# Counting a group's destination nodes from any 32-node quarter, and summing its messages by 32 columns of the array

## The chip, the cores and the metric

The kernel runs on one core of a Trainium2 chip. The metric is the device time of one execution in microseconds (us); the median of three executions of the kernel before is 4363.7 us (4302.89 to 4385.22). The profile is of another single execution, whose span is 3774.9 us; that is some 589 us shorter than the median, and no view of the profile says where the timed executions spend the difference.

## What is computed

Four graph layers in a row work on 6250 nodes with 64 features and 206,250 edges, sorted by destination node. Three of them are sums over neighbours with fixed weights. The third of the four, in which the change lies, makes a message for each edge from the edge's own 64 attributes and from the features of its source node, and takes the root of the mean of the squared messages at each destination:

```python
x = jax.nn.relu(E @ mlp_w1 + mlp_b1)
x = jax.nn.relu(x @ mlp_w2 + mlp_b2)
scale = jax.nn.sigmoid(x @ Bw + Bb)
shift = x @ Cw + Cb
msg = scale * Vp[src] + shift
M = jnp.power(jnp.clip(msg, EPS, None), ALPHA)
ssum = jax.ops.segment_sum(M, dst, num_segments=n)
```

## The kernel before

The nodes are padded to 49 blocks of 128 (`NB = 49`, `P = 128`), in 7 chunks of 7 blocks. Layers one, two and four multiply by a dense adjacency matrix `A`, which the kernel builds in the first 680 us and keeps in memory; their matmuls are those of `spread` (L732), with 64 columns of the TensorE array for each and two column halves in turn. The third layer is a stage of its own, from L1039 on, and the profile has it from 1125 to 3280 us.

That stage goes through 202 groups of 1024 edges (`G`, `J = 8` edges for each of 128 partitions). For each group g:

- GpSimd (POOL) issues 8 indirect DMAs (L1195), one for each j, which fetch the rows of `Vp_dram` of 128 source nodes into the tile `v`. `v` has four buffers.
- TensorE transposes the edge attributes (L1203), runs the two small layers (L1207, L1211) and the products that give scale and shift (L1216, L1220); ScalarE evicts in between.
- VectorE forms the message from `gate`, `v` and the shift (L1225 to L1227); ScalarE squares it, and VectorE and ScalarE split the square into three bfloat16 parts `m3` (L1229 to L1233), 192 values for an edge.
- VectorE makes `to` (L1238): for each edge a row of zeros with a one at its destination, as a comparison of a counter `count` with `rel_b`, the destination less the group's origin.
- TensorE sums the messages by destination (L1246): `to` is the stationary operand, 128 edges by 128 nodes, `m3` the moving one, and the sums of a block of 128 nodes collect in one PSUM bank, `acc[b]`. When the last group that may lead to a block is through, VectorE reduces the three parts into `H` (L1250), and after seven blocks `finished` does the rest for a chunk.

The edges are sorted, so a group of 1024 edges leads to about 31 nodes in a row. `window(g)` gives a range that holds them, with 32 nodes to spare at either end, and it counts in whole blocks of 128: of the 202 groups, 150 have a window of two blocks and 52 of one. So `to` has 2048 or 1024 elements in each partition, and L1246 runs 16 or 8 matmuls; 2816 in all.

Between the groups, `some_of` deals out other work: comparisons of blocks of A with their transposes (`crossed`, L1136 and L1139) and partial sums for the fourth layer (`partial`, L732 and L1152). The text of the loop isn't the order of the instructions: the framework's scheduler moves them on each engine, so that TensorE's work for group g+1 stands among that for group g. [...]

Ahead of the stage, GpSimd fills `origin` and `width` (L1082) with one memset for each run of groups of the same value, and VectorE subtracts the origin from all destinations (L1085 to L1093) and counts those that fall outside their window in `missed`; if there were any, another program (`general`) would do the whole work again.

Of the kernel before, what the change touches and what calls it, by code (L numbers as in the profile page):

```python
# [9 lines left out]
BF16 = mybir.dt.bfloat16  # L10
# [3 lines left out]
OP = mybir.AluOpType  # L14
AX = mybir.AxisListType

P = 128
N = 6250
D = 64
NB = 49  # L20
NP = NB * P
CB = 7
NC = NB // CB
W = CB * P
E = 206250
J = 8
# [564 lines left out]
CW = 448  # L591
CS = NP // CW
SG = 8
DRIFT = 32


def window(g):

    per = N / E
    lo = max(int(g * P * J * per) - DRIFT, 0) // P  # L600
    hi = min(int((g + 1) * P * J * per) + DRIFT, NP - 1) // P
    return lo, hi - lo + 1


# [1 line left out]
def fast(ctx, tc, bad, x, src, dst, edge_attr, W3, b3, W4, b4, w1, b1, w2, b2, Bw, Bb, Cw, Cb,  # L606
         pAw, pAb, pBw, pBb, out):

    nc = tc.nc
# [129 lines left out]
    with ExitStack() as ph:  # L739

        ipool = ph.enter_context(tc.tile_pool(name="ipool", bufs=1))
        with ExitStack() as first:
# [11 lines left out]
            hi = dpool.tile([P, K1], I32, name="hi")  # L754
# [14 lines left out]
        count = ipool.tile([P, 128, GQ], BF16, name="count")  # L769
# [40 lines left out]
        with ExitStack() as ps:  # L810
# [18 lines left out]
            for c in range(GC):  # L829
# [13 lines left out]
                for k in range(2):  # L843
# [8 lines left out]
                                    op=OP.add)  # L852
# [65 lines left out]
            for s in range(CS):  # L918
                strip = spool.tile([P, NB, CW], BF16, name="strip")
                for q in range(NQ):  # L920
                    at = (s * CW // 2) + q * GB
                    lo = opool.tile([P, GB // GQ, 128, GQ], BF16, name="lo")
                    hd = opool.tile([P, GB // GQ, 2 * NB, GQ], BF16, name="hd")
                    for t, of, k in ((hd, turns, 0), (lo, count, 1)):
# [114 lines left out]
    with ExitStack() as ph:  # L1039
        cpool = ph.enter_context(tc.tile_pool(name="cpool", bufs=1))  # L1040
# [34 lines left out]

        origin = tpool.tile([P, G], F32, name="origin")
        width = tpool.tile([P, G], F32, name="width")
        for t, value in ((origin, lambda g: window(g)[0] * P), (width, lambda g: window(g)[1] * P)):
            g0 = 0
            for g in range(1, G + 1):  # L1080
                if g == G or value(g) != value(g0):
                    nc.gpsimd.memset(t[:, g0:g], float(value(g0)))  # L1082
                    g0 = g
        rel = tpool.tile([P, G, J], F32, name="rel")
        nc.vector.tensor_tensor(rel, dst_g, origin.unsqueeze(2).to_broadcast([P, G, J]),  # L1085
                                op=OP.subtract)
        rel_b = cpool.tile([P, G, J], BF16, name="rel_b")
# [4 lines left out]
        nc.vector.tensor_add(off, off, rel)  # L1092
        nc.vector.tensor_reduce(missed[:, 1:2], off.rearrange("p g j -> p (g j)"), axis=AX.X,  # L1093
                                op=OP.add)
        count = cpool.tile([P, 2 * P, J], BF16, name="count")
        nc.gpsimd.iota(count, pattern=[[1, 2 * P], [0, J]], base=0, channel_multiplier=0,
                       allow_small_or_imprecise_dtypes=True)

        before.close()
        mpool = ph.enter_context(tc.tile_pool(name="mpool", bufs=3))  # L1100
# [53 lines left out]
        todo, crossings = [], []  # L1154
# [13 lines left out]
        def some_of(left):  # L1168

            n = -(-len(todo) // max(left, 1))  # L1170
            for _ in range(n):
                f, *args = todo.pop(0)
                f(*args)
# [13 lines left out]

        plan(FIRST, False)
        last = {b: g for g in range(G) for b in range(window(g)[0], sum(window(g)))}
        ends = [last[c * CB + CB - 1] for c in range(NC)]  # L1190
        acc = {}
        for g in range(G):
            v = mpool.tile([P, J, D], F32, name="v", bufs=4)
            for j in range(J):
# [20 lines left out]
            for b in range(2):  # L1215
                nc.tensor.matmul(p_bc[:, 4 * b:4 * b + 4].rearrange("p j o f -> p (j o f)"), ones,  # L1216
                                 BC_b, start=True, stop=False)
                for k in range(2):
                    q = 2 * b + k
# [13 lines left out]
            nc.vector.tensor_sub(m3[:, :, 2, :], m, m3[:, :, 1, :])  # L1233

            some_of(min(k for k in ends if k >= g) + 1 - g)
            b0, nb = window(g)
            to = mpool.tile([P, 2 * P, J], BF16, name="to")
            nc.vector.tensor_tensor(  # L1238
                to[:, :nb * P, :], count[:, :nb * P, :],
                rel_b[:, g, :].unsqueeze(1).to_broadcast([P, nb * P, J]), op=OP.is_equal)  # L1240
            for b in range(b0, b0 + nb):
                begins = b not in acc
                if begins:
                    acc[b] = ps_s.tile([P, 512], F32, name="p_s")
                for j in range(J):
                    nc.tensor.matmul(acc[b][:, :3 * D], to[:, (b - b0) * P:(b - b0 + 1) * P, j],  # L1246
                                     m3[:, j].rearrange("p t f -> p (t f)"),
                                     start=(begins and j == 0), stop=(last[b] == g and j == J - 1))
                if last[b] == g:
                    nc.vector.tensor_reduce(  # L1250
                        H[:, b, :], acc[b][:, :3 * D].rearrange("p (t f) -> p f t", f=D),
                        axis=AX.X, op=OP.add)
                    if b % CB == CB - 1:
                        finished(b // CB)

        assert not todo and len(crossings) == 28 * CB


        nc.vector.tensor_reduce(missed[:, 2:3], unlike, axis=AX.X, op=OP.add)
# [12 lines left out]
    with ExitStack() as ph:  # L1272
# [5 lines left out]
        for layer in range(3):  # L1278
# [78 lines left out]
```

## Time and profile before

| | |
|---|---|
| median time, three executions | 4363.7 us |
| span of the profiled execution | 3774.9 us |
| busy: PE, DVE, ACT, POOL | 3173.7, 1845.4, 1329.9, 1723.4 us |
| third layer's stage (first to last fetch of `v`) | 1125 to 3280 us, 202 groups |
| granted TensorE clock, whole span | 0.933 |
| L1238 `to` | 202 instructions, 218.8 us |
| L1246 sums by destination | 2816 matmuls |

PE is TensorE's matmuls, PEld its weight loads, DVE VectorE, ACT ScalarE, POOL GpSimd, SP SyncE. A row of a group names the line, the engine, the operation, the tile written and the tiles read, the shape (partitions x elements), and the count; after the bar stand the busy time in us, the mean duration of one in ns, and the idle time of the engine just ahead of these instructions with what ended it. Where matmuls overlap, the mean duration of one is longer than the time from one to the next. "issue" is time in which an engine waited for nothing that the profile shows.

### The profile page before, as it was taken

The numbers are of one execution on the slowest core, as the hardware profiler recorded it, in microseconds if no ns is written. First come the engines' busy times: TensorE is split into PE (matmuls) and PEld (weight loads), VectorE is DVE, ScalarE is ACT, GpSimd is POOL, SyncE is SP. The second block draws the span as 40 slices with busy tenths as digits, with TensorE's granted clock in tenths as the row PEclk, the third lists the DMA queues.
The fourth block names the chain that finished last, engine by engine and source line by source line (L and its number), as shares of the span: only waits on it lengthen the run. The fifth ranks groups of instructions, "written<-read, shape, count | busy, mean of one in ns | idle before, by whom it ended". The sixth has DMA issues, their size and how long they took to land.

```text
span 3774.9 us, 59396 instructions
## 1 busy us (share of the span) xinstructions
PE 3173.7 (84%) x24499; PEld 1907.5 (51%) x24499; DVE 1845.4 (49%) x3013; ACT 1329.9 (35%) x2120; POOL 1723.4 (46%) x1822
## 2 busy tenths in 40 slices
PE   0499998999967777888878888888888888799999
PEld 0366665555534444444544444454444454466665
DVE  5999992221124445555555554555555455430000
ACT  0477771100104434334434434443443434310000
POOL 4100000000017777777777777777777777500000
PEclk9999998999978889889989889889899999899999
DMA  3244446968894333343434334333233333499987
GB/s 108 80 181 180 180 180 276 421 276 347 315 168 128 85 81 104 82 129 90 119 100 120 101 99 127 93 114 112 81 112 116 104 113 93 142 338 376 371 352 298
DMA packets 278031, 650.47 MB, mean 172 GB/s; under 512 B 106505, under 2 KB 158787, under 8 KB 275699
## 3 DMA queue, kind: packets, MB, share of 16 engines
q1 hardware_dynamic: 220036, 584.91, 42.9%
q0 software_dynamic: 54112, 58.92, 7.3%
q8 instruction: 194, 3.18, 0.3%
q10 hardware_dynamic: 3600, 2.73, 0.3%
q14 instruction: 89, 0.73, 0.1%
HBM read 562.82 MB, written 83.58 MB: 171 GB/s over the span
## 4 chain that ended last, share of the span: by engine, by line
POOL 32%; PE 15%; issue 12%; DMA 8%; DVE 2%; ACT 1%; POOLq 0%; DVEq 0%
POOL v L1195 32%; PE p_sum L732 11%; DMA v<-Vp_dram,src_g 7%; PE p_node L723 1%; PE p_bc L1220 1%; DMA piece<-A 1%; PE p L1207 1%; PE p L1211 0%; PE p_s L1246 0%; DVE m L1225 0%; PE p_sum L1136 0%; DVE junk L1139 0%; PE p_bc L1216 0%; DVE m L1226 0%; DVE m L1231 0%
## 5 line engine op out<-in xcount | busy, mean ns | idle before, releaser
L1195 POOL DMA_INDIRECT v<-Vp_dram,src_g x1616 | 1662.5, 1029 | 528.3 <-issue 455.2
L732 PE MATMUL p_sum<-piece,U 128*64 128x448 bf16 x10290 | 1083.7, 359 | 46.3 <-DVE junk L1139 22.9
L732 PEld LDWEIGHTS <-U 128*64 128x64 bf16 x12348 | 688.1, 111 | 610.8 <-issue 172.2
L1220 PE MATMUL p_bc<-BC,h 128*128 128x256 f32 x1616 | 507.5, 437 | 19.1 <-ACT h L1213 18.8
L1082 POOL MEMSET origin<- 128x4 f32 (+3 forms) x49 | 1.7, 100 | 968.3 <-PE p_sum L732 968.3
L1225 DVE TENSOR_TENSOR m<-gate,v 128x512 f32<-128x512 f32 x202 | 139.6, 691 | 510.9 <-DMA v<-Vp_dram,src_g 424.5
L1220 PEld LDWEIGHTS p_bc<-BC,h 128*128 128x128 f32 x1616 | 300.3, 207 | 173.7 <-issue 84.8
L1246 PE MATMUL p_s<-m,to 128*128 128x192 bf16 x2816 | 293.0, 259 | 73.8 <-DVE m L1233 73.7
L1246 PEld LDWEIGHTS <-to 128*128 128x128 bf16 x2816 | 270.6, 147 | 130.8 <-issue 124.3
L938 ACT ACTIVATE strip<-p_a 128x784 bf16<-128x784 f32 x392 | 301.6, 820 | 90.9 <-PE p_a L934 89.5
L1216 PE MATMUL p_bc<-BC_b,ones 3*128 3x512 bf16 x404 | 168.7, 418 | 190.0 <-DVE m L1226 188.4
L1229 ACT ACTIVATE m<-m 128x512 bf16<-128x512 f32 x202 | 126.9, 628 | 444.2 <-DVE m L1227 443.6
L1238 DVE TENSOR_TENSOR to<-count,rel_b 128x2048 bf16<-128x2048 bf16 (+1 forms) x202 | 218.8, 1084 | 101.8 <-PE p_s L1246 100.7
L973 ACT ACTIVATE y<-p_sum 128x448 f32<-128x448 f32 x56 | 30.5, 544 | 674.8 <-PE p_sum L732 674.8
L1207 PE MATMUL p<-eT,w_d 128*128 128x512 f32 x404 | 246.8, 696 | 25.3 <-ACT eT L1205 24.9
L1139 DVE SCALAR_TENSOR_TENSOR junk<-p_sum,there 128x896 bf16<-128x896 bf16 x196 | 213.1, 1087 | 78.6 <-PE p_sum L1136 69.9
L1211 PE MATMUL p<-h,w_d 128*128 128x512 f32 x404 | 240.7, 680 | 8.3 <-ACT h L1209 7.3
L1223 ACT ACTIVATE gate<-p_bc 128x512 f32<-128x512 f32 x202 | 120.6, 597 | 351.3 <-PE p_bc L1220 351.1
L925 DVE TENSOR_TENSOR lo<-count,key 128x2048 bf16<-128x2048 bf16 x196 | 238.2, 1215 | 0.0
L732 PE MATMUL p_sum<-strip,U 128*64 128x448 bf16 x2058 | 236.6, 358 | 0.4 <-ACT strip L938 0.4
L1231 DVE TENSOR_TENSOR m<-m,m 128x512 f32<-128x512 f32 x202 | 139.7, 691 | 168.8 <-ACT m L1230 168.8
L934 PE MATMUL p_a<-hd,lo 128*128 128x98 bf16 x3136 | 190.2, 214 | 33.1 <-DVE lo L925 31.8
(173 smaller groups left out, 3012.8 us busy)
## 6 DMA issues: line engine op xcount, KB each, us to landing
piece<-A SPq DMA_DIRECT2D x498, 784.0 KB
A<-strip SPq DMA_DIRECT2D x14, 5488.0 KB
e<-in_edge_attr SPq DMA_DIRECT2D x202, 256.0 KB
v<-Vp_dram,src_g POOLq DMA_INDIRECT x1616
there<-A SPq DMA_DIRECT2D x56, 448.0 KB
there<-A SPq DMA_DIRECT2D x56, 336.0 KB
pairs<-pair SPq DMA_DIRECT2D x1, 1616.0 KB
Vp_dram<-v SPq DMA_DIRECT2D x7, 224.0 KB
```

What stands on the lines that cost most here:

```text
L732: nc.tensor.matmul(p[half * D:(half + 1) * D, :w], U3[:, b, k, :], at_block, start=(i < 2), stop=(i >= 3 * n - 2))
L925: nc.vector.tensor_tensor(t, of.unsqueeze(1).to_broadcast(t.shape), key[:, k, at:at + GB].rearrange("p (h j) -> p h j", j=GQ) .unsqueeze(2 ...
L934: nc.tensor.matmul(p[:, j, :2 * NB], lo[:, g // GQ, :, g % GQ], hd[:, g // GQ, :, g % GQ], start=True, stop=True)
L938: nc.scalar.activation(strip[:, :, col:col + 2 * SG].rearrange("p b (j l) -> p b j l", l=2), p[:, :, :2 * NB].rearrange("p j (b l) -> p b ...
L1139: nc.vector.scalar_tensor_tensor(junk, p.rearrange("p a q -> p (a q)"), 0.0, held["there"][:, b % ROWS].rearrange("p h w -> p (h w)"), op0 ...
L1195: nc.gpsimd.indirect_dma_start(out=v[:, j, :], out_offset=None, in_=Vp_dram[:, :], in_offset=bass.IndirectOffsetOnAxis(ap=src_g[:, g, j:j ...
L1207: nc.tensor.matmul(p_1, w1_d, eT, start=True, stop=True)
L1211: nc.tensor.matmul(p_2, w2_d, h1, start=True, stop=True)
L1216: nc.tensor.matmul(p_bc[:, 4 * b:4 * b + 4].rearrange("p j o f -> p (j o f)"), ones, BC_b, start=True, stop=False)
L1220: nc.tensor.matmul(p_bc[:, 2 * q:2 * q + 2].rearrange("p j o f -> p (j o f)"), h2[:, q * P:(q + 1) * P], BC, start=False, stop=(k == 1))
L1238: nc.vector.tensor_tensor(to[:, :nb * P, :], count[:, :nb * P, :], rel_b[:, g, :].unsqueeze(1).to_broadcast([P, nb * P, J]), op=OP.is_equal)
L1246: nc.tensor.matmul(acc[b][:, :3 * D], to[:, (b - b0) * P:(b - b0 + 1) * P, j], m3[:, j].rearrange("p t f -> p (t f)"), start=(begins and j ...
```

## The change

Windows are counted in quarters of a block, `Q = 32` nodes. A window may begin at any quarter and has at most four of them (the `assert`), so `to` and `count` shrink from 256 to 128 nodes. By the same formula as before, 193 groups have four quarters, eight have three and one has two. Each quarter gets a matmul of its own for each j: 32 columns of `to` are stationary, and the result goes to the 32 partitions of `acc` that belong to the quarter, so that four matmuls in a row use four different column groups of the array. Their number is 6384. The loop over j is now outside the one over the quarters. The number of blocks that a group touches, of PSUM tiles and of reductions (L1250) stays. Its purpose is to stop comparing with, and multiplying by, nodes to which a group can't lead.

```diff
+Q = 32
 def window(g):
     per = N / E
-    lo = max(int(g * P * J * per) - DRIFT, 0) // P
-    hi = min(int((g + 1) * P * J * per) + DRIFT, NP - 1) // P
+    lo = max(int(g * P * J * per) - DRIFT, 0) // Q
+    hi = min(int((g + 1) * P * J * per) + DRIFT, NP - 1) // Q
+    assert hi - lo < P // Q
     return lo, hi - lo + 1
...
-        count = cpool.tile([P, 2 * P, J], BF16, name="count")
-        nc.gpsimd.iota(count, pattern=[[1, 2 * P], [0, J]], base=0, channel_multiplier=0,
+        count = cpool.tile([P, P, J], BF16, name="count")
+        nc.gpsimd.iota(count, pattern=[[1, P], [0, J]], base=0, channel_multiplier=0,
...
-            b0, nb = window(g)
-            to = mpool.tile([P, 2 * P, J], BF16, name="to")
+            q0, nq = window(g)
+            to = mpool.tile([P, P, J], BF16, name="to")
             nc.vector.tensor_tensor(
-                to[:, :nb * P, :], count[:, :nb * P, :],
-                rel_b[:, g, :].unsqueeze(1).to_broadcast([P, nb * P, J]), op=OP.is_equal)
-            for b in range(b0, b0 + nb):
-                begins = b not in acc
-                if begins:
+                to[:, :nq * Q, :], count[:, :nq * Q, :],
+                rel_b[:, g, :].unsqueeze(1).to_broadcast([P, nq * Q, J]), op=OP.is_equal)
+            for b in range(q0 // QB, (q0 + nq - 1) // QB + 1):
+                if b not in acc:
                     acc[b] = ps_s.tile([P, 512], F32, name="p_s")
-                for j in range(J):
-                    nc.tensor.matmul(acc[b][:, :3 * D], to[:, (b - b0) * P:(b - b0 + 1) * P, j],
+            for j in range(J):
+                for q in range(q0, q0 + nq):
+                    at = q % QB * Q
+                    nc.tensor.matmul(acc[q // QB][at:at + Q, :3 * D],
+                                     to[:, (q - q0) * Q:(q - q0 + 1) * Q, j],
                                      m3[:, j].rearrange("p t f -> p (t f)"),
-                                     start=(begins and j == 0), stop=(last[b] == g and j == J - 1))
-                if last[b] == g:
+                                     start=(q not in begun and j == 0),
+                                     stop=(last[q] == g and j == J - 1))
+            begun.update(range(q0, q0 + nq))
+            for b in range(q0 // QB, (q0 + nq - 1) // QB + 1):
+                if last[b * QB + QB - 1] == g:
                     nc.vector.tensor_reduce(
```

`QB = P // Q` is four. `origin` and `width` are filled from `window(g)[0] * Q` and `window(g)[1] * Q`.

More of the change, by code (lines that the diff above doesn't have):

```diff
@@ L1077, in fast @@
         width = tpool.tile([P, G], F32, name="width")
-        for t, value in ((origin, lambda g: window(g)[0] * P), (width, lambda g: window(g)[1] * P)):
+        for t, value in ((origin, lambda g: window(g)[0] * Q), (width, lambda g: window(g)[1] * Q)):
             g0 = 0
@@ L1189, in fast @@
         last = {b: g for g in range(G) for b in range(window(g)[0], sum(window(g)))}
-        ends = [last[c * CB + CB - 1] for c in range(NC)]
-        acc = {}
+        QB = P // Q
+        ends = [last[(c + 1) * CB * QB - 1] for c in range(NC)]
+        acc, begun = {}, set()
         for g in range(G):
@@ L1254, in fast @@
                         finished(b // CB)
-        assert not todo and len(crossings) == 28 * CB
         nc.vector.tensor_reduce(missed[:, 2:3], unlike, axis=AX.X, op=OP.add)
```

## The prediction

> **What bounds the kernel now.** The change touches only the third layer's stage, so I read first what ends last there. The page's chain of waits comes first, then its busy tenths in 40 slices.
>
> ```profile
> POOL 32%; PE 15%; issue 12%; DMA 8%; DVE 2%; ACT 1%; POOLq 0%; DVEq 0%
> PE   0499998999967777888878888888888888799999
> POOL 4100000000017777777777777777777777500000
> PEclk9999998999978889889989889889899999899999
> ```
>
> The first line is the chain by engine: 32% POOL, 12% "issue" and 8% DMA are one thing, the fetches of `v` and the spaces between them. The slices show TensorE full on both sides of the stage and at seven to eight tenths in it, and POOL steady at 7. A POOL that is 70% busy looks free; its groups of instructions say otherwise. The third and fourth lines below are the same view with shapes kept apart, over 1125 to 3280 us.
>
> ```profile
> L1195 POOL DMA_INDIRECT v<-Vp_dram,src_g x1616 | 1662.5, 1029 | 528.3 <-issue 455.2
> L1246 PE MATMUL p_s<-m,to 128*128 128x192 bf16 x2816 | 293.0, 259 | 73.8 <-DVE m L1233 73.7
> L1238 DVE TENSOR_TENSOR to<-count,rel_b 128x2048 bf16<-128x2048 bf16 x150 | 183.2, 1222 | 81.1 <-PE p_s L1246 80.6
> ...
> L1238 DVE TENSOR_TENSOR to<-count,rel_b 128x1024 bf16<-128x1024 bf16 x51 | 34.9, 687 | 20.7 <-PE p_s L1246 20.1
> ```
>
> 1616 fetches of 1029 ns fill 1663 us; before nearly every one stand 0.30 us of "issue". 1616 x (1.029 + 0.305) = 2156 us, which is the whole stage (3280 - 1125 = 2155). I went through the gaps between the fetches: all are 304 to 316 ns, so POOL never waits for a buffer or for another engine. It sets the stage, 10.67 us for a group. TensorE's sum over the same window is 1776.8 us busy, so it has 378 us to spare.
>
> Next, why 1029 ns, where the median fetch takes 947? The timeline of POOL and VectorE at one place:
>
> ```profile
> 2013.48 0.95 POOL L1195 DMA_INDIRECT v<-Vp_dram,src_g  x1 [0.30 <-issue]
> 2014.63 1.23 DVE L1238 TENSOR_TENSOR to<-count,rel_b 128x2048 bf16<-128x2048 bf16 x1 [2.27 <-PE p_s L1246]
> 2014.73 1.95 POOL L1195 DMA_INDIRECT v<-Vp_dram,src_g  x1 [0.30 <-issue]
> 2016.98 0.94 POOL L1195 DMA_INDIRECT v<-Vp_dram,src_g  x1 [0.30 <-issue]
> ```
>
> The fetch that starts 0.1 us after `to` takes 1.95 us in place of 0.95. It ends 0.82 us after `to` ends. In the trace nearly all fetches that a `to` prolongs end 0.81 to 0.82 us after it: they stand still while `to` runs. `to` is on no engine's critical list, yet it delays the engine that is.
>
> **What the Trainium skill says.** (1) SBUF — State Buffer, "Who interferes with whom": a VectorE instruction with two SBUF inputs contends with a GpSimd instruction that reads SBUF, and the later one blocks in full. The page infers that generating descriptors is not held up by `tensor_tensor`; the trace differs, 1.95 against 0.95 us, and decides. (2) TensorE: Matmul & The Clock Gate, "Part 3: Packing small matmuls": matmuls on different 32-column groups run side by side, started about 4 ns apart, 2.38 times the rate for three of them. The trace has no 32-column matmul; its 64-column ones of L732 start in pairs 3 ns apart, then 186 ns on, which agrees. (3) TensorEngine Tiling (Array Packing), "Key Properties": changing the tiling mode drains the array. From the timeline, two L1220 (216 ns from start to start) begin at 2004.68 and L732 follows at 2005.24, so the switch cost about 0.13 us. (4) TensorE's page again, "Part 1: The HAM clock gate": after an idle window the clock is halved. The trace has 0.50 in 2032 to 2036 us, after TensorE had done little for 6 us.
>
> **The change, part by part.**
>
> *`to` on VectorE.* Before: 150 x 1.222 + 52 x 0.687 = 219 us. After: 193 groups have 128 nodes by 8 edges, the 1024-element form that is in the profile, 0.687 us; the nine smaller ones about 0.55. 193 x 0.687 + 9 x 0.55 = 138 us. 81 us less VectorE work, all of it beside POOL's list, worth nothing by itself.
>
> *What `to` costs POOL.* The excess of all fetches is 1616 x (1.029 - 0.947) = 132 us. I gave each `to` the excess of the fetch that it overlaps: the 148 long ones of 1.22 us cost 557 ns each (82 us), the 52 short ones 125 ns each (6.5 us), 89 us together with three odd ones. The rest, 43 us, goes with L1231, L1233 and the like, and stays. That a `to` of half the length costs a quarter or less is as it should be: it meets a fetch's beginning half as often and holds it half as long. After: 202 x 125 ns = 25 us. POOL's list gets shorter by 89 - 25 = 64 us, and it is the list that sets the stage. Bounds: if the new schedule puts `to` at worse moments, 250 ns each, 38 us; if none collides, 89 us. I take 64.
>
> *The sums on TensorE.* Before, start to start is 83 ns (192 columns moving), 13.94 matmuls for a group: 1.16 us. After, 31.6 matmuls. If four column groups run side by side as two do in L732, a j costs about 83 + 3 x 3 = 92 ns, 8 x 92 = 0.74 us, plus two mode switches of 0.13 where the neighbours are full-width matmuls: 1.00 us. If they overlap so far as loads and issue allow, the nearest row is L934, a load and a matmul every 47 ns: 31.6 x 47 + 260 = 1.75 us. If they don't overlap, 31.6 x 83 = 2.62 us. I take 1.00, 0.16 us less for a group, 32 us of TensorE in the stage, hidden behind POOL. The middle value adds 119 us, which also fits into the 378 spare.
>
> *Weight loads* go from 2816 to 6384 of a quarter of the columns; L732's loads of 64 columns also start 3 ns apart, so I charge nothing beyond the above.
>
> *The loop order* lets a finished block's L1250 wait for the other block's matmuls as well, at most 0.7 us, 49 times. Behind it on VectorE stand the next group's L1225 or L1238; POOL has four buffers of `v`, so nothing of it reaches POOL. Nothing.
>
> *Ahead of the stage*: the iota shrinks (3.75 us), and the memsets of `origin` become more, those of `width` fewer. POOL is through with them at 1089 us and then waits for VectorE's `missed` (35.9 us, till 1124.9), whose work doesn't change. Nothing.
>
> Sum: 64 us. Off the timed median: 4363.7 - 64 = 4300 us, 1.5% less. I carry the saving over in microseconds[...].
>
> **The rivals.**
>
> *Rival 1, TensorE sets the stage when it is timed.* For it: the timed executions are 589 us longer than the profiled one, and the profile has spells at half clock; a TensorE granted less would reach POOL's pace. Against: the profiled stage has no trace of it. At half clock, 13.94 x 166 = 2.31 us before against 8 x 175 + 260 = 1.66 after: 0.65 x 202 = 131 us, so 4233 us; with part of the 64 on top, 4170 to 4230.
>
> *Rival 2, the narrow matmuls don't overlap.* 2.62 - 1.16 = 1.46 us more for a group, 295 us of TensorE work. Busy 1777 + 295 = 2072 of 2155 us, with idle spells that the data forces; TensorE then sets the pace. Taking TensorE's present share of stalls (378 us) as half avoidable: 2072 + 189 = 2261, 106 us more, about 4470 us. Against it speak L732's pairs. This one is slower.
>
> *Rival 3, the gain is hidden.* POOL gains, but messages arrive no sooner: VectorE's L1225 waits 424.5 us for `v` in all, so most groups do follow POOL; but where they trail it by up to 7.8 us in the trace, the other engines pace. Then a third of the gain may stay: 4340 us.
>
> **How the numbers follow.** My forecast has 0.42, rival 1 0.31, rival 2 0.15, rival 3 0.12. The three executions of before differ by 1.9%, so the forecast and rival 3 spill over the 2% bounds (4276 and 4451 us): of their 0.54, 0.09 to the faster side and 0.03 to the slower. Rival 1 lies mostly beyond, 0.28 of 0.31, and rival 2 with 0.14 of 0.15. That gives faster 0.37, same 0.46, slower 0.17. The range goes from rival 1's lower end, 4170, to 4430, which leaves out rival 2 and little else.
>
> **What would show it.** In the changed kernel's profile L1238 has to have 1024 elements and 0.69 us; the mean fetch should fall from 1029 to about 989 ns with the median at 947 and the space at 0.30; the stage should last about 2091 us. The matmuls to `p_s` should start in fours a few ns apart, with some 90 ns from one four to the next; 47 ns or more between all of them would speak for the middle value, 83 for rival 2. If POOL shows gaps beyond 0.32 us, it no longer sets the stage and the forecast is wrong. If the profile's span falls by 64 us and the timed median by twice that, it was rival 1.

## The result, and the profile after

The changed kernel takes 4570.54 us (median of four executions, 4565.64 to 4606.45), the kernel before beside it 4373.69 us (four, 4302.89 to 4385.22). The ratio is 1.0565, 95% interval 1.0409 to 1.0722: the change makes the kernel slower by 5.6%, where 1.5% faster was forecast. Ratios here and below are of the fast executions alone, those within 1.5% of the fastest of the same kernel, so this one isn't the 1.045 of the two medians. The profiled execution has a span of 4563.9 us, so this time the profile shows what was timed.

The page of the changed kernel: busy tenths in 40 slices, the chain of waits by engine, and three groups of instructions.

```profile
PE   0699989996566656667676667766666776679999
POOL 4000000001565555555455545545545555420000
PEclk9999989997687777777777777777877877789999
...
PE 11%; DVE 1%; another core or an unknown queue 0%; DMA 0%; issue 0%; ACT 0%; DVEq 0%
...
L1198 POOL DMA_INDIRECT v<-Vp_dram,src_g x1616 | 1575.7, 975 | 1364.7 <-DVE m L1228 811.4
...
L1241 DVE TENSOR_TENSOR to<-count,rel_b 128x1024 bf16<-128x1024 bf16 (+2 forms) x202 | 137.8, 683 | 728.7 <-remote 607.5
L1251 PE MATMUL p_s<-m,to 128*32 128x192 bf16 x6384 | 238.3, 277 | 186.2 <-DVE m L1236 110.7
```

GpSimd (POOL) was at a steady 7 and is at 5; TensorE was at 8 and is at 6 to 7; the granted clock is 0.76 to 0.79 in the stage, against 0.89 to 0.92 in the first profile. No engine is full. The chain adds up to 12% of the span: it breaks off at a release that the profile doesn't show, which is itself a sign. The fetches did get shorter (975 ns for 1029), and so did `to` (0.683 us); but GpSimd, which never waited in the first profile, now waits 811 us for VectorE to give a buffer of `v` back. The list of waits (engine, line, what it waited for: us in total, times, longest) names the next link:

```profile
POOL v L1198 <- DVE m L1228: 811.4, 121, 15.6
DVE to L1241 <- remote: 607.5, 68, 16.1
...
ACT h L1212 <- remote: 203.4, 18, 23.9
```

"remote" is written where the releasing event isn't in the trace; there is no other core here. `to` waits for TensorE to be through with an older `to`, and L1212 for the matmul L1210. So the waits lead to TensorE. What one of them looks like, from the timeline of all engines (start, duration, engine, line):

```profile
2837.23 0.66 PE L1206 MATMUL p_e<-ident,e 128*128 128x128 f32 x4
2837.63 0.94 POOL L1198 DMA_INDIRECT v<-Vp_dram,src_g  x1 [0.30 <-issue]
2838.88 0.94 POOL L1198 DMA_INDIRECT v<-Vp_dram,src_g  x1 [0.30 <-issue]
...
2848.87 0.94 POOL L1198 DMA_INDIRECT v<-Vp_dram,src_g  x1 [0.30 <-issue]
2851.11 0.69 DVE L1241 TENSOR_TENSOR to<-count,rel_b 128x1024 bf16<-128x1024 bf16 x1 [14.71 <-remote]
2851.72 0.42 DVE L1230 TENSOR_SCALAR m<-m 128x512 f32<-128x512 f32 x1
2852.51 0.69 ACT L1212 ACTIVATE h<-p,b_c 128x512 f32<-128x512 f32 x1 [16.77 <-remote]
2853.10 0.62 ACT L1232 ACTIVATE m<-m 128x512 bf16<-128x512 f32 x1
2853.25 2.08 PE L1214 MATMUL p<-h,w_d 128*128 128x512 f32 x2 [15.37 <-ACT h L1212]
```

By the ends that the trace gives, TensorE had done its work by 2837.9 us. ScalarE and VectorE, which need nothing but that, begin over 13 us later; TensorE then waits for ScalarE. Only GpSimd goes on, until it has no buffer left. I call this a stand-still. The ends of matmuls in a trace are modelled, so it can't be told here whether the work itself ended late or the news of its end came late. The second picture is TensorE inside its sums:

```profile
2502.15 0.72 PE L1251 MATMUL p_s<-m,to 128*32 128x192 bf16 x23
...
2503.51 0.24 PE L1251 MATMUL p_s<-m,to 128*32 128x192 bf16 x1 [0.64 <-issue]
...
2504.24 0.29 PE L1251 MATMUL p_s<-m,to 128*32 128x192 bf16 x1 [0.48 <-issue]
...
2504.93 0.32 PE L1251 MATMUL p_s<-m,to 128*32 128x192 bf16 x1 [0.41 <-issue]
```

Twenty-three matmuls run at full pace, then the rest come one by one, about 0.70 us from start to start or a multiple of it, with "issue" before each: TensorE waits for nothing that the profile shows. I call these steps.

To measure both over the whole stage I counted, in each trace, the stretches of over 3 us in which none of TensorE, VectorE and ScalarE starts anything, the 0.70- or 1.40-us spaces between TensorE's starts, and TensorE's semaphore updates that come over 1 us after the modelled end of the instruction that makes them ("late"). The stage runs from the first fetch of `v` to the start of the last message; in the three kernels below that have no fetches it is counted from the first message, some 17 us after the first transfer of `v`. The rest of the span is 1617 to 1640 us in every kernel below and is not discussed.

One fact on the chips is needed to read the numbers. The experiments ran on five chips. On four of them the kernel before takes 4339.01, 4341.92, 4351.24 and 4346.98 us (39, 7, 7 and 11 executions), as in the times that the prediction started from. On the fifth, which served the runs e13 to e16, it takes 3776.66 us (7 executions, 3773.62 to 3783.75), as in the profile that the prediction read. I call it the quiet chip. Each chip served on one occasion only, so the runs don't tell what belongs to a chip from what belongs to the occasion. Times are compared with the kernel before on the same chip.

### The profile page after: what moved, and what is told of

Read it like the earlier page. It is cut to its first block, busy times and chain, and to the rows that moved or that the text cites. A ratio compares the mean times of both kernels' runs of the same rounds, so it can differ in the third digit from the quotient of the medians.

```text
span 4563.9 us, 66598 instructions
## 1 busy us (share of the span) xinstructions
PE 3366.5 (74%) x28067; PEld 1887.0 (41%) x28067; DVE 1771.7 (39%) x3013; ACT 1323.2 (29%) x2120; POOL 1636.8 (36%) x1886
## 5 line engine op out<-in xcount | busy, mean ns | idle before, releaser
L1198 POOL DMA_INDIRECT v<-Vp_dram,src_g x1616 | 1575.7, 975 | 1364.7 <-DVE m L1228 811.4
L734 PE MATMUL p_sum<-piece,U 128*64 128x448 bf16 x10290 | 1141.1, 365 | 153.9 <-issue 59.6
L1223 PE MATMUL p_bc<-BC,h 128*128 128x256 f32 x1616 | 550.5, 460 | 120.9 <-issue 66.1
L1241 DVE TENSOR_TENSOR to<-count,rel_b 128x1024 bf16<-128x1024 bf16 (+2 forms) x202 | 137.8, 683 | 728.7 <-remote 607.5
L1251 PE MATMUL p_s<-m,to 128*32 128x192 bf16 x6384 | 238.3, 277 | 186.2 <-DVE m L1236 110.7
L1210 PE MATMUL p<-eT,w_d 128*128 128x512 f32 x404 | 290.4, 808 | 98.8 <-ACT eT L1208 84.3
L1138 PE MATMUL p_sum<-ident_b,piece 128*128 128x128 bf16 (+1 forms) x1568 | 154.5, 252 | 241.7 <-issue 115.6
L1251 PEld LDWEIGHTS <-to 128*32 128x32 bf16 x6384 | 178.0, 143 | 300.2 <-issue 297.9
L1138 PEld LDWEIGHTS <-piece 128*128 128x128 bf16 (+1 forms) x1568 | 124.1, 119 | 327.5 <-issue 318.8
L1212 ACT ACTIVATE h<-p,b_c 128x512 f32<-128x512 f32 x202 | 138.4, 685 | 406.5 <-remote 203.4
L1216 ACT ACTIVATE h<-p,b_c 128x512 f32<-128x512 f32 x202 | 138.3, 685 | 279.7 <-remote 131.8
```

The lines of the kernel that those rows point to most:

```text
L734: nc.tensor.matmul(p[half * D:(half + 1) * D, :w], U3[:, b, k, :], at_block, start=(i < 2), stop=(i >= 3 * n - 2))
L1138: nc.tensor.transpose(p[q, a, :], held[half][:, a, lo:lo + q.stop - q.start], ident_b)
L1198: nc.gpsimd.indirect_dma_start(out=v[:, j, :], out_offset=None, in_=Vp_dram[:, :], in_offset=bass.IndirectOffsetOnAxis(ap=src_g[:, g, j:j ...
L1210: nc.tensor.matmul(p_1, w1_d, eT, start=True, stop=True)
L1212: nc.scalar.activation(h1, p_1, AF.Relu, bias=b1_c)
L1223: nc.tensor.matmul(p_bc[:, 2 * q:2 * q + 2].rearrange("p j o f -> p (j o f)"), h2[:, q * P:(q + 1) * P], BC, start=False, stop=(k == 1))
```

## The experiments

### The kernel before, in an execution as it is timed

e1_before is the kernel before, unchanged.

> The kernel before, unchanged, to see its profile at the time that it usually has (4303 to 4385 us), where the first profile had 3775. Theory A (TensorE's completions are delivered late, by an amount that grows with the number of its instructions, in both kernels): about 4360 us, and the profile shows stretches of 5 to 15 us in which TensorE, VectorE and ScalarE all stand still, as in the changed kernel, some 590 us of them in the stage; granted clock well below 0.93. Theory B (the 32-column matmuls bring the stalls): no such stretches, and what makes 4360 us of 3775 must be something else, such as slower fetches.

It took 4346.43 us (20 executions, ratio 1.0012, 0.9984 to 1.0039). Its page and its list of waits:

```profile
PE   0599989999367576677667677766766777789999
POOL 4000000000467665656556565665656656600000
PEclk9999999999578787888788888878887978889999
...
L1195 POOL DMA_INDIRECT v<-Vp_dram,src_g x1616 | 1631.6, 1010 | 1087.7 <-DVE m L1225 570.4
```

```profile
POOL v L1195 <- DVE m L1225: 570.4, 96, 16.5
...
DVE to L1238 <- remote: 263.5, 38, 20.3
```

The profile on which the prediction rests shows none of this: GpSimd steady at 7, no wait for a buffer. The two spans differ by 568 us, of which 559 lie in the third layer's stage: 2716 us here, 2157 there. In these 559 us, TensorE's gaps of over 3 us make up 390 and its busy time 135, while its granted clock in the stage falls from 0.90 to 0.81. The stand-stills, in which all three engines start nothing, are the larger part of those gaps; the steps are too few here to matter. Theory A asked for some 590 us of stand-stills; there are 326. In numbers:

| | stage us | TensorE instructions (matmuls and loads) | stand-stills | steps | late updates, of those recorded |
|---|---|---|---|---|---|
| before, first profile | 2157 | 19,555 | 10, 37 us | 18 | 2 of 2412 |
| e1_before | 2716 | 19,555 | 49, 326 us | 43 | 324 of 2200 |
| after | 2939 | 26,659 | 63, 448 us | 282 | 357 of 2250 |

So GpSimd doesn't set the stage where it was timed. What a fetch saves there is only a longer wait for a buffer.

### Which part of the change costs: the short comparison or the narrow sums

e2_slide keeps the short `to` and goes back to matmuls of 128 columns, as many as before, by writing the comparison into the middle of a buffer of zeros and sliding the window over it. e4_eight keeps the short `to` and makes one 128-column matmul for each j.

```diff
-            to = mpool.tile([P, P, J], BF16, name="to")
+            to = slid[g % 3]
...
+            for b in range(q0 // QB, (q0 + nq - 1) // QB + 1):
+                c0 = P - Q + b * P - q0 * Q
+                for j in range(J):
+                    nc.tensor.matmul(acc[b][:, :3 * D], to[:, c0:c0 + P, j],
```

> The changed kernel's short comparison of 128 nodes, but written into the middle of a buffer of zeros, so that each block is summed with 128-column matmuls as before (2816 of them, 5632 TensorE instructions, no 32-column ones). Theory A: TensorE has as many instructions as before, so about the time of before, less up to 64 us that the fetches no longer wait for the comparison: 4290 to 4370 us. Theory B: without the 32-column matmuls the stalls go, and what my prediction said of the short comparison comes true: 4300 us or less.

> The changed kernel's windows and short comparison, with a single 128-column matmul for each of the 8 edges of a partition (1616 in all), into the sums of the window's first block; this leaves out the part of the sums that belongs to the second block and puts rows into wrong places. 2400 TensorE instructions fewer than before. Theory A: some 75 to 90 us less than the second kernel of this series, 4200 to 4290 us. Theory B: the same as the second kernel within 20 us.

e2_slide: 4410.49 us, ratio 1.0104 (0.9984 to 1.0223), not to be told from no change. e4_eight: 4326.22 us, 0.9964 (0.9932 to 0.9996), with 17,155 TensorE instructions in the stage. Both are above what theory A gave them. The short comparison alone brings next to nothing and doesn't cost the 5.6%. e2_slide's stage is 2795 us, 79 over e1_before with the same number of instructions; I have no cause for that, and don't read differences of that size in what follows.

e3_split takes the kernel before and splits only its matmuls, each into four of 32 columns, so `to` stays long and the windows whole blocks.

```diff
                 for j in range(J):
-                    nc.tensor.matmul(acc[b][:, :3 * D], to[:, (b - b0) * P:(b - b0 + 1) * P, j],
+                    for q in range(4):
+                        at = q * 32
+                        nc.tensor.matmul(acc[b][at:at + 32, :3 * D],
+                                         to[:, (b - b0) * P + at:(b - b0) * P + at + 32, j],
```

> The kernel before with its wide windows and its wide comparison, and each of the 2816 matmuls by destination done as four of 32 columns (11,264, so 16,900 TensorE instructions more than before). Theory A: the changed kernel lost some 200 us with 7136 instructions more (and gained up to 64 by the comparison), 31 to 37 ns for each; 16,900 of them give 520 to 630 us, so 4890 to 5000 us. Theory B: the stalls come with the 32-column mode itself, once for each group, so about as in the changed kernel, 4570 to 4650 us.

4869.24 us, ratio 1.1222 (1.1121 to 1.1323). The stage is 3241 us, 525 more than e1_before, and the steps are 856; the stand-stills are fewer (31, 180 us, against 49 and 326). The row of the sums in e1_before, then in e3_split:

```profile
L1246 PE MATMUL p_s<-m,to 128*128 128x192 bf16 x2816 | 314.8, 270 | 115.3 <-DVE m L1233 85.4
...
L1248 PE MATMUL p_s<-m,to 128*32 128x192 bf16 x11264 | 533.9, 291 | 567.1 <-issue 491.4
```

The busy time rose by 219 us, but the idle time before these matmuls rose from 115 to 567 us, 491 of it "issue". The narrow sums alone, without any other part of the change, make the kernel slower, by the waiting between them more than by their own length.

### Narrow, or only many

e8_one_by_one is the changed kernel with its two loops exchanged: eight matmuls in a row go to the same 32 columns, so that none runs beside the next. e5_halves and e6_sixtyfour are the kernel before with each matmul cut in two, by the moving operand (2 x 96 columns, at full array width) or by the array (2 x 64 columns).

```diff
-            for j in range(J):
-                for q in range(q0, q0 + nq):
+            for q in range(q0, q0 + nq):
+                for j in range(J):
```

```diff
                 for j in range(J):
-                    nc.tensor.matmul(acc[b][:, :3 * D], to[:, (b - b0) * P:(b - b0 + 1) * P, j],
-                                     m3[:, j].rearrange("p t f -> p (t f)"),
+                    for h in range(2):
+                        cols = slice(h * 96, h * 96 + 96)
+                        nc.tensor.matmul(acc[b][:, cols], to[:, (b - b0) * P:(b - b0 + 1) * P, j],
+                                         m3[:, j].rearrange("p t f -> p (t f)")[:, cols],
```

> The changed kernel with its two loops swapped: all eight matmuls of one quarter, then those of the next. The number of TensorE instructions and their 32-column mode stay; but matmuls in a row use the same columns of the array, so they can't run side by side, some 83 ns each and 2.6 us for a group in place of 0.75. Theory A1 (count of instructions): not faster than the changed kernel's 4570 us, rather 4600 to 4700 us for the longer sums. Theory A2 (side by side is what hurts): the steps of 0.70 us go, and the time falls below the changed kernel's, 4400 to 4500 us, although the sums take more TensorE time.

> The kernel before, and each matmul by destination done as two, both with all 128 columns of the array, each with 96 of the 192 moving columns: 5632 TensorE instructions more, none of them in a column tile, none beside another. Theory A1 (each further TensorE instruction costs some 31 ns in late completions, whatever its kind): 5632 x 31 = 175 us, so about 4515 us. Theory A2 (it is the matmuls that run side by side in column tiles, and end together, that make TensorE stop and go at steps of 0.70 us): 4340 to 4380 us, no more steps of 0.70 us in the sums by destination than in the kernel before.

> The kernel before, and each matmul by destination done as two of 64 columns, which run side by side: the same 5632 TensorE instructions more as in the kernel with halves of the moving operand. Theory A1: the same as that one, about 4515 us. Theory A2: steps of 0.70 us in the sums by destination, and a time between that of the kernel with halves and that of the one with four of 32 columns (4869 us): about 4500 us if it goes by the count of column-tile matmuls, and clearly above the kernel with halves.

| | time us | ratio, interval | TensorE instructions in the stage | stage us | ns of stage for each instruction over e1_before's |
|---|---|---|---|---|---|
| after | 4570.54 | 1.0565 (1.0409 to 1.0722) | 26,659 | 2939 | 223 us / 7104 = 31 |
| e8_one_by_one | 4664.0 | 1.0713 (1.0642 to 1.0784) | 26,659 | 3015 | 299 / 7104 = 42 |
| e5_halves | 4593.73 | 1.0532 (1.0459 to 1.0605) | 25,171 | 2986 | 270 / 5616 = 48 |
| e6_sixtyfour | 4528.11 | 1.0372 (1.0295 to 1.0450) | 25,171 | 2914 | 198 / 5616 = 35 |
| e3_split | 4869.24 | 1.1222 (1.1121 to 1.1323) | 36,403 | 3241 | 525 / 16,848 = 31 |

Full-width matmuls cut in two cost as much for each further instruction as the 32-column ones, so it isn't the narrow mode. Nor is it a failing overlap: in e8_one_by_one the sums start 69 ns apart in the median, where most of the changed kernel's start within 6 ns of the one before, and the stage is longer by 76 us only, no more than e2_slide's unexplained 79. The number of TensorE instructions is what they have in common. It isn't an exact price: 31 to 48 ns by the stages, 28 to 45 by the times against the kernel before on the same chip, and e4_eight's 2400 fewer gave back 22 us of e1_before's stage, 9 ns each, but 101 us of e2_slide's, which has the same comparison, 42 ns each. e5_halves took 79 us more than the 4515 that the count alone had given.

### What the price hangs on

e7_plainload is the kernel before with `v` brought by one plain transfer of SyncE; e9_after_plain the changed kernel and e10_split_plain the split, treated in the same way.

```diff
-            for j in range(J):
-                nc.gpsimd.indirect_dma_start(
-                    out=v[:, j, :], out_offset=None, in_=Vp_dram[:, :],
-                    in_offset=bass.IndirectOffsetOnAxis(ap=src_g[:, g, j:j + 1], axis=0))
+            nc.sync.dma_start(
+                v, Vp_dram[:P * J, :].rearrange("(p j) f -> p j f", j=J))
```

> The kernel before without GpSimd's 1616 indirect fetches: v is loaded for each group with one plain transfer from the SyncE queue, of the first 1024 rows of Vp_dram in every group; this leaves out the gather by source node, so the messages are of wrong nodes. It asks what the stage's base state, with completions of TensorE that come up to 15 us late, hangs on. Theory F (the fetches, with their descriptors and semaphore traffic, are what delays them): the stretches in which TensorE, VectorE and ScalarE all stand still go, and the stage falls to TensorE's own 9 to 10 us for a group, some 3600 us in all. Theory G (TensorE's instructions alone do it, in this mix with short matmuls): the stage stays within 5% of 2716 us, about 4300 us.

> The changed kernel with v brought by one plain transfer of SyncE per group instead of eight indirect fetches of GpSimd. It leaves out the gather: every group gets the first 1024 rows of Vp. The kernel before, treated so, has taken 3309 us and a stage of 1669 us. Theory I (the price of a further TensorE instruction in the stage, 31 ns, is paid only while the indirect fetches run beside it): about the same time, 3290 to 3350 us, since the narrow sums then cost what they take side by side, under 1 us per group, and the ratio of 1.056 between the two kernels is gone. Theory P (each further instruction costs by itself, whatever GpSimd does): 7104 more instructions at 31 ns give 220 us more, about 3530 us.

> The kernel before with each 128-column matmul of the sums split into four of 32 columns (the split that took 4869 us with the fetches, 530 us over the kernel before), and with v by one plain transfer per group; it leaves out the gather. Theory I: 3300 to 3450 us, the split's 16,848 further instructions being hidden or nearly so. Theory P: 3309 plus 530, about 3840 us. The 0.70-us steps between sums, 687 in the split with fetches, are gone by I and stay by P.

| | with the fetches: time, stage, late | without: time, stage, late |
|---|---|---|
| before | 4346.43, 2716, 324 | 3309.25, 1669, 2 |
| after | 4570.54, 2939, 357 | 3256.39, 1614, 2 |
| split | 4869.24, 3241, 253 | 3399.06, 1758, 2 |

Steps are counted over the whole stage here; the 687 in the expectation above are those between the sums alone. The row of the sums in e7_plainload, then three lines of the page of e9_after_plain:

```profile
L1244 PE MATMUL p_s<-m,to 128*128 128x192 bf16 x2816 | 272.6, 248 | 10.3 <-DVE m L1231 10.2
...
PE   0299999899999599999999999999999999899999
...
PEclk9999999899999799999999999999999999899999
...
L1249 PE MATMUL p_s<-m,to 128*32 128x192 bf16 x6384 | 182.1, 255 | 8.3 <-DVE m L1234 8.2
```

Without indirect fetches there are 2 late updates, no stand-still over 3 us, and five steps or fewer. TensorE is full in the stage and its clock is at 9. The changed kernel's stage is 55 us *shorter* than that of the kernel before, although it has the same 7104 instructions more; the sums are busy 182.1 us (0.90 us for a group), and 272.6 in e7_plainload. The split pays 89 us for 16,848 instructions, 5 ns each. These three ran on chips where the kernel before took 4341.92 and 4351.24 us beside them. The changed kernel is faster than either theory had it. So the price of 31 ns is not TensorE's own: it is there only together with the indirect fetches. Whether it is their transfers or GpSimd's work of starting them, these runs don't tell apart.

e12_pool_busy was to tell GpSimd's being busy from the transfers: the plain load, and eight unused iotas for each group.

```diff
+            for j in range(J):
+                idle = mpool.tile([P, 512], BF16, name="idle")
+                nc.gpsimd.iota(idle, pattern=[[1, 512]], base=0, channel_multiplier=0,
+                               allow_small_or_imprecise_dtypes=True)
```

> The kernel before with v by one plain transfer per group (it leaves out the gather), and with eight iotas of 128x512 on GpSimd per group in the place of the fetches, about 0.95 us each, their result unused: GpSimd is about as busy as with fetches, but starts no transfers. Theory T (the transfers of the indirect fetches, or their issue, bring the late completions): 3310 to 3360 us and almost no late completions of TensorE. Theory G (GpSimd's being busy, or its semaphore traffic and its use of the memory beside VectorE, brings them): over 3800 us, with late completions by the hundred.

It took 4121.98 us, and by neither theory's way. Nothing tied the iotas to the groups, so GpSimd ran all 1616 in one row of some 0.8 ms; and the first two clips of a message that VectorE began beside them (L1229, 421 ns in the median) took 29.9 us and 783.6 us, the second one to the end of that row (durations: min, median, max in ns):

```profile
L1229 DVE TENSOR_SCALAR m<-m x202: 415/421/783619, 1147.2 to 3628.1; 128x512 f32<-128x512 f32 x101
```

Two stand-stills make up 806 us, and 4118.2 - 806 = 3312 is close to the span of e7_plainload, 3306.3; late updates: 2. On the question it was made for it says little.

### Fewer fetches, smaller fetches, fewer buffers

e11_half (before) and e13_after_half (after) keep four of the eight fetches, e14_six (before) six, the rest of `v` being a plain transfer. e15_rows (before) keeps all eight, of 32 rows each. e16_two is the changed kernel with two buffers of `v` in the place of four.

```diff
+            nc.sync.dma_start(
+                v[:, J // 2:, :], Vp_dram[:P * J // 2, :].rearrange("(p j) f -> p j f", j=J // 2))
-            for j in range(J):
+            for j in range(J // 2):
```

```diff
-                    out=v[:, j, :], out_offset=None, in_=Vp_dram[:, :],
-                    in_offset=bass.IndirectOffsetOnAxis(ap=src_g[:, g, j:j + 1], axis=0))
+                    out=v[:32, j, :], out_offset=None, in_=Vp_dram[:, :],
+                    in_offset=bass.IndirectOffsetOnAxis(ap=src_g[:32, g, j:j + 1], axis=0))
```

```diff
-            v = mpool.tile([P, J, D], F32, name="v", bufs=4)
+            v = mpool.tile([P, J, D], F32, name="v", bufs=2)
```

> The kernel before with four of the eight indirect fetches of each group; the other half of v comes by a plain transfer, so half of the gather is left out. GpSimd then needs at most 808 fetches by 1.3 us, 1050 us, and can't set the stage. Theory F (each fetch disturbs TensorE for itself): the stage goes about half of the way from 2716 us to 1669 us, 2190 us, time about 3800 us. Theory S (any stream of fetches turns the stage over to the slow state): the stage stays above 2500 us, time above 4100 us. Theory C (it is GpSimd being the limit that makes the stage long, and nothing else): 3310 us, as without fetches, since GpSimd now needs less than the other engines.

> The changed kernel with four of the eight indirect fetches of each group, the other half of v by a plain transfer (half of the gather is left out). The kernel before, treated so, took 3421 us (stage 1800 us). Theory N (the price of a further TensorE instruction comes up only where the fetches fill GpSimd's time): 3360 to 3420 us, the change being faster or even, as it is without fetches (3256 to 3309). Theory H (the price goes with the number of fetches): half of 31 ns for 7104 instructions, 110 us more, about 3530 us.

> The kernel before with six of the eight indirect fetches of each group, the last two columns of v by a plain transfer (a quarter of the gather is left out). Six need 1212 times 1.33 us, 1610 us of GpSimd, still under the 1669 us that the stage takes without fetches. Theory N (trouble comes where the fetches fill GpSimd's time): a stage of 1850 to 2050 us, time 3480 to 3680 us. Theory H (it goes with the number of fetches, on a line through four and eight): stage 2260 us, time 3880 us.

> The kernel before with eight indirect fetches per group of 32 rows each instead of 128; the other 96 partitions of v come by a plain transfer (three quarters of the gather are left out). Theory R (the rows and their packets do the harm): hardly any late completions; if a fetch of 32 rows still occupies GpSimd 0.95 us with 0.3 us between, 1616 of them need 2030 us and the time is 3650 to 3750 us, if it is shorter the time is under 3600 us. Theory K (the number of fetch instructions on GpSimd does it): a stage above 2500 us, over 4150 us, with late completions by the hundred.

> The changed kernel with two buffers for v instead of four: all fetches, but GpSimd can run at most two groups ahead. Theory A (fetches that run ahead in a dense row do the harm): less than 4500 us. Theory W (GpSimd's running ahead is what lets it use the stand-stills of the others, the harm being the same): 4570 us or more, by up to 200 us.

| | chip, before beside it | time us | stage us | late updates |
|---|---|---|---|---|
| e11_half | 4351.24 | 3421.41 | 1800 | 55 |
| e13_after_half | quiet, 3776.66 | 3246.97 | 1630 | 2 |
| e14_six | quiet | 3343.56 | 1721 | 2 |
| e15_rows | quiet | 3656.79 | 2037 | 2 |
| e16_two | quiet | 3718.94 | 2100 | 2 |

e11_half, on a chip with late updates, is the only one of these that says something of them: half of the fetches give a sixth of the late updates, and 115 of the 1030 us that eight fetches add to the stage (counted from the first transfer of `v` in all three kernels). It is far from half the way, so the harm doesn't go with the number of fetches alone, and none of the three theories fits. The others met no late updates to explain, because their chip has none even with all fetches; what I meant to learn from them on the cause was not learned. e13_after_half and e14_six come in below both of their theories, whose figures came from the other chips. The runs on this chip show something else: with all eight fetches, GpSimd's list sets the stage, as the prediction had it:

```profile
L1197 POOL DMA_INDIRECT v<-Vp_dram,src_g x1616 | 1540.1, 953 | 528.0 <-issue 468.3
```

This row of e15_rows gives 1616 x (0.953 + 0.305) = 2033 us, and the stage is 2037. And e16_two is the changed kernel where it can work as meant. Its slices and its row of fetches:

```profile
POOL 4100000000006777777777777777777777500000
...
L1198 POOL DMA_INDIRECT v<-Vp_dram,src_g x1616 | 1603.8, 992 | 527.7 <-issue 444.0
```

GpSimd is at a steady 7 again and waits for no buffer: 1616 x (0.992 + 0.305) = 2096 us, and the stage is 2100. Against the kernel before on the same chip the ratio is 0.9848 (0.9832 to 0.9865), 58 us less; the stage is 57 us shorter than in the first profile, and 1616 fetches shorter by 37 ns are 60 us. It differs from the changed kernel in its buffers too; the changed kernel with four was not run on this chip, and e16_two on no other, so no version is shown to beat both.

### The result once more

e17_after is the changed kernel, e18_split the split, both again.

> The changed kernel as it is. If the kernel before beside it takes about 3777 us (TensorE's completions not late): theory Q (GpSimd's fetches then set the stage, the saving on `to` counts in full, and the narrow sums are hidden) 3700 to 3730 us, a ratio of 0.980 to 0.988, the stage some 60 us under 2157; theory P (each of the 7104 further instructions costs 31 ns wherever it runs) 3930 us. If the kernel before takes about 4350 us: 4570 us again.

> The kernel before with each 128-column matmul of the sums split into four of 32 columns, as in e3_split. If the kernel before beside it takes about 3777 us: theory Q 3760 to 3800 us, since without fetches the split's stage was 1758 us, under the 2157 that the fetches need; theory P 3777 plus 530, 4300 us. If the kernel before takes about 4350 us: about 4870 us again.

It was a chip of the other kind (before 4346.98 us): 4559.23 us, ratio 1.0492 (1.0447 to 1.0537), and 4868.83 us, 1.1205 (1.1148 to 1.1263). The stages are 2940 and 3246 us, with 265 and 870 steps: the loss repeats on another chip, and so does its form.

## Why the prediction was wrong

*The step that failed first: "POOL never waits for a buffer or for another engine. It sets the stage".* That is right of the execution that was profiled, and of the quiet chip. In the executions that were timed GpSimd waits 570 us for buffers before the change and 811 after it. Of the 64 us some 55 were won (the fetches' excess over 945 ns is 104 us in e1_before and 49 after), and they lay off the path. The prediction's own test says so: "If POOL shows gaps beyond 0.32 us, it no longer sets the stage". The 589 us between profile and median were the warning. I gave them to one rival instead of asking what kind of execution would be timed.

*The second: the sums at "0.16 us less for a group", the weight loads at nothing.* As durations they were about right: 32 matmuls to `p_s` take 0.89 us where nothing breaks them up (the changed kernel at 2835.04 us, with 83 ns from one four to the next where 92 were worked out), forecast 1.00. But the price of 7104 further instructions was not in their duration. It was 31 ns each in this stage, 223 us: TensorE's busy time rose by 55 us, its gaps of 0.3 to 1 us by 80 and those of over 3 us by 79. "It has 378 us to spare" counted idle time as if any instruction could use it.

*`to` on VectorE* came out as worked out: 137.8 us for 138, 0.683 us for 0.687.

*What `to` costs GpSimd*: mean fetch forecast at 989 ns. 992 in e16_two, where GpSimd's list is the path, and a stage shorter by 57 us makes a kernel faster by 58. So the mechanism and the size held on the quiet chip; 64 was 7 too many.

*Rival 1*, TensorE setting the stage in the timed executions, had the right place and the wrong means: it made matmuls longer at half clock, and so narrow sums cheaper. The granted clock was 0.76 to 0.79, and most of the time is lost between instructions. *Rival 2* came nearest with 4470 us, by a mechanism that wasn't there: e8_one_by_one removes the overlap and loses 76 us of stage on top, while the rest of the loss stands without that. *Rival 3* had it right that the gain on the fetches would be hidden, but not that the change would cost more than it hides.

*What stays open.* Shown: the further TensorE instructions cost 31 ns and more each only where the indirect fetches run too (with fetches, 4346 us becomes 4570 by the change and 4869 by the split; without, 3309 becomes 3256 and 3399), and the loss was seen only on chips that aren't the quiet one. Not shown: how a fetch delays TensorE's work or the news of its end, why one chip has none of it, and what the 0.70 us are. The transfers themselves are not slower: the packets of the indirect queue take 79 ns in the mean in the first profile's stage, 82 in the changed kernel's and 71 in e17_after's. Nor do the packets that bring TensorE's instructions fall into the stand-stills: of 105 large ones in the changed kernel's stage none begins in one, where chance would give 16.

One rival is untested: the recording itself. Each timed execution on record has a span and a granted clock of its own, so none is known to have run unrecorded, and that a profile agrees with the other executions says nothing against it. In every trace that has late updates by the dozen, records of updates of TensorE, VectorE and ScalarE are missing: after the change 2281 are recorded for VectorE, against 2676 in the first profile, and e1_before has 2200 of the 2412 that TensorE makes. Where TensorE isn't late, as without fetches or on the quiet chip, at most 1% of them are missing. Late in turn are TensorE's updates alone; no recorded one of VectorE or ScalarE in the stage comes over 1 us after the last instruction that makes one. Against a simple link speaks e11_half, which has only 2182 of TensorE's 2412 records but little of the loss. Whether an execution that isn't recorded would lose the same time is open.

## What to carry to other kernels

Here the span of the profile was 589 us under the time that was measured, and it was a profile of another kind of execution. Where the two differ, profile the unchanged kernel again before an argument rests on which engine never waits. Price TensorE's instructions by number as well as by length where a stage runs beside indirect fetches: cutting matmuls into pieces cost 31 to 48 ns here for each further instruction, so twice that for a piece with its load, even where the pieces overlapped. And compare on more than one chip, since the same change was worth -58 us (with two buffers) on one and +197 to +212 us on others.

## What the hardware showed that I had not expected

- In the presence of indirect fetches, on four of the five chips, TensorE's updates of semaphores come over 1 us after the modelled ends of its instructions, one in seven in e1_before and one in six after the change, there up to 16 us late; without the fetches or on the fifth, 2 of some 2400. The recording may have a part in this.
- An indirect fetch of 32 rows occupies GpSimd nearly as long as one of 128: 866 ns in the median in e15_rows, against 947 in the first profile (means 953 and 1029).
- A VectorE clip of 421 ns in the median took 783.6 us while GpSimd ran iotas back to back (e12_pool_busy): it ended with the last of them. The one before it got through after 29.9 us.
